# A quarter of some softmax subtractions on ACT and POOL, attention keys spread by DMA, and transposes moved ahead on TensorE

## The chip, the cores and the metric

The kernel runs on one core of a Trainium2 chip. The metric is the device time of one execution in microseconds. The engines are named as in the profile: PE (TensorE), DVE (VectorE), ACT (ScalarE), POOL (GpSimd) and SP (SyncE, which here only issues DMA transfers). All arithmetic is in float32.

## The reference

A sequence of 128 batches of 64 tokens with 128 channels goes through four layers. What matters here are their five attentions, each with 16 heads of 8 channels over 64 keys: L0s (self) and L0c (against a context), L1c (context), L2s (self) and L2c (context). After L0c and after L2c comes an MLP; L3 is a mixture of three experts that the change doesn't touch. Cut to one attention:

```python
def _attend(q, k, v):
    attn = jnp.einsum('bhnd,bhsd->bhns', q, k) * SCALE
    attn = jax.nn.softmax(attn, axis=-1)
    o = jnp.einsum('bhns,bhsd->bhnd', attn, v)
    return o.transpose(0, 2, 1, 3).reshape(B, N, D)
...
xm = _ln(x) * (1.0 + sc_sa) + sh_sa
qkv = (xm @ qkv_w + qkv_b).reshape(B, N, 3, H, HD)
...
x = x + g_sa * (_attend(q, k, v) @ sa_proj_w + sa_proj_b)     # L0s
x = x + _attend(q, k, v) @ ca_proj_w + ca_proj_b              # L0c: k, v from the context
```

The gates (`g_sa` and the like) are rows of one value per batch and channel, computed once from a condition vector.

## The kernel before

**Tiling.** The 8192 tokens are 16 groups (`NST`) of 8 batches, that is 512 tokens. A group's activations x stay in SBUF as 128 tokens by 4 tiles by 128 channels. Each attention stage runs over the 16 groups, one after the other, and the five stages follow in the order above. The list of all groups of a run of stages is what `attend` gets as `ats`.

**Halves and steps.** The scores of a group are computed in two halves of 4 batches, u = 0 and u = 1. `step(k)` emits one half's worth of work, and it does so for three halves at once: the scores of half k (`scores`), the transposes and exponentials of half k-1 (`turned`, twice, for the first and the second pair of head groups), and the weighted sums of half k-2 (`weighted`). In between it advances two lists of generators: `prepare` (for later groups: load, statistics, norm, transposes `psT`, their eviction into `cm` or `xm`, the key product `pk`, the query product `pq`, the value product `pvv`) and `finish` (for earlier groups: sums of the exponentials, their reciprocals, the output projection `py` and the addition into x). Each `go(prep, i)` or `go(fin, i)` runs a generator to its next `yield`. The schedule is manual: every engine executes its instructions in the order in which they are written out, and waits at an instruction whose semaphores aren't there, with all that follows on that engine behind it.

**Scores.** 16 heads are 4 groups g of 4 heads j. The keys of a group lie 4 times in `kbd`, once for each head j, with the rows of the other heads zero: POOL makes them with four products by a mask of 0 and 1 (L444). The scores `sc` take 4 banks of PSUM, 2048 columns, one bank for each g; there is one such buffer. DVE takes the maximum of each row of 64 (`mx`, L485) and subtracts it into SBUF (`e`, L487). PE turns `e` by transposes (`pp`, L503; 2 banks, one buffer), ACT takes the exponential while it evicts them (`eT`, L507), and PE multiplies with the values `vbd` (`po`, L520), which carry a column of ones for the sums.

**PSUM.** Of the 8 banks, 4 are `sc`, 2 `pp`, and 2 are the pool `mm`, from which `po`, `pk`, `pq`, `psT`, `pvv` and `py` all take their buffers. A new tile there waits until the tile that had its bank before has been read out.

**Eviction of the transposes.** In self groups and in L1c ACT evicts `psT` in eight pieces with scale and bias of the batch (L359, 2.47 us for the eight); in L0c and L2c it is one copy (L379, 0.58 us).

**Finish.** SP moves the rows of sums to DRAM (`sums`) and back with another shape (`rc`), and moves half of `o` to other partitions (L545, four transfers). DVE takes the reciprocal, `recs` goes to DRAM, and `rb` comes back broadcast over the channels of each head (L554); self groups also load a tile of gates (`gt`, L278). POOL multiplies (`oT`, L557), PE projects (`py`, L563), and DVE adds into x (L565 in cross groups; L568 and POOL in self groups).

**The first microseconds.** Weights and x come in by one queue on SP; DVE makes the statistics and the norm of the first group, and the products with the mask.

Of the kernel before, what the change touches and what calls it, by code (L numbers as in the profile page):

```python
# [15 lines left out]
P = 128  # L16
NST = 16
TT = 4
# [17 lines left out]
for _name, _n in _VECS:  # L36
# [13 lines left out]
    "L3_xcond_router_W": (3, 3), "L3_xcond_e_w1": (9, 256), "L3_xcond_e_w2": (6, 128),  # L50
    "L3_xcond_gate_w1": (3, 128), "L3_xcond_gate_w2": (1, 128), "L3_xcond_out_w": (1, 128),
}
_RAW = [
    "x", "cond_1024", "ctx_1024", *_WTS,
    "L0_xcond_ca_proj_b", "L1_xcond_bp", "L2_xcond_b_cproj", "L3_xcond_router_b", "L3_xcond_e_b2",
# [4 lines left out]
def tile_kernel(ctx: ExitStack, tc: tile.TileContext, a: dict, out: bass.AP):  # L60
# [15 lines left out]
    nc.sync.dma_start(cond, a["cond_1024"])  # L76
    vec_rows = const([_NVEC, P], "vec_rows")
    nc.scalar.dma_start(vec_rows, a["vecs"])
    mask = const([P, 4], "mask")
    nc.scalar.dma_start(mask, a["mask"])  # L80

    w = {}

    def load_weights(prefix, pool=cp):
        for name, (k, n) in _WTS.items():
            if name.startswith(prefix):
                t = pool.tile([P, k, n], F32, tag=name, name=name)
                src = a[name]
                if len(src.shape) == 3:
                    src = src.rearrange("e c n -> (e c) n")  # L90
                nc.sync.dma_start(t, src.rearrange("(k p) n -> p k n", p=P))
                w[name] = t

    xs = [const([P, TT, P], f"x{s}") for s in range(NST)]
# [23 lines left out]

    ident = const([P, P], "ident")
    make_identity(nc, ident)  # L120
    nhalf = const([P, TT], "nhalf")
    G.memset(nhalf, -0.5)

# [43 lines left out]
        Places.ak.tile([P, NB, 8, 32], F32, tag=f"vbd{i}", name=f"vbd{i}", bufs=1) for i in range(2)  # L167
    ]

    def clear(t):  # L170
        G.memset(t, 0.0)
        G.memset(t[0:L, :, :, 16:17], 1.0)
        G.memset(t[L:P, :, :, 17:18], 1.0)


# [2 lines left out]
    condT = const([P, P], "condT")  # L178
    scT = const([P, P], "scT")
    mods = {}  # L180

    def col(name, i=0):
        r = _ROW[name] + i
# [20 lines left out]

    def folded_column(wp, bp, bv, i):
        pb = mm("pb")
        T.matmul(pb[:, 0:1], w[wp][:, 0], col(bv, i), start=True, stop=True)
        t = const([P, 1], "pb_" + wp)
        V.tensor_add(t, pb[:, 0:1], col(bp))
        proj_bias[wp] = t  # L210
# [3 lines left out]
    def gate_table(wmod, wp, i=2, bias=None):  # L214

        table = dp.tile([P, 2, P], F32, tag="gate_" + wp, name="gate_" + wp)
        rows = const([P, 2, P], "gate_rows")
        gb = const([P, P], "gate_bias")
        V.tensor_scalar_mul(gb, mods[wmod][:, i, :], proj_bias[wp] if bias is None else bias)

        def second():
            pg = mm("pg")
            for q, src in enumerate((mods[wmod][:, i, :], gb)):
                T.transpose(pg[:, ts(q, P)], src, ident)
            V.tensor_copy(rows, pg[:, 0 : 2 * P].rearrange("p (i c) -> p i c", i=2))
            nc.sync.dma_start(table, rows)
            gates[wp] = table

        return second

    def folded_row(wp, bp, bv):
        bvs = const([P, P], "bvs")
        V.tensor_copy(bvs, col(bv, 1).broadcast_to([P, P]))

        def second():
            pb = mm("pb")
            T.matmul(pb[:, :P], bvs, w[wp][:, 0], start=True, stop=True)
            V.tensor_add(row_bias[bp], row_bias[bp], pb[:, :P])
            proj_bias[wp] = row_bias[bp]

        return second

    def condition():
        pc = mm("pc")
        T.transpose(pc[:, :P], cond, ident)
        V.tensor_copy(condT, pc[:, :P])
        S.activation(scT, pc[:, :P], AF.Silu)
        pv = mm("pv")
        T.transpose(pv[:, :_NVEC], vec_rows, ident[:_NVEC, :_NVEC])
        V.tensor_copy(vec, pv[:, :_NVEC])  # L250
        V.tensor_scalar_add(vec1, vec, 1.0)

    first_mods = modulations("L0_xcond_adaln_w", "L0_xcond_adaln_b", 6, (1, 4))
# [19 lines left out]
    def gate_tile(pool, s, wp):  # L273

        gt = pool.tile([P, TT, 2, P], F32, tag="gt", name="gt")
        for h in range(2):
            r = gates[wp].rearrange("(s t h) i c -> s h t (i c)", t=TT, h=2)[s, h]
            nc.sync.dma_start(  # L278
                gt[ts(h, L)].rearrange("p t i c -> p t (i c)"),
                r.unsqueeze(0).broadcast_to([L, TT, 2 * P]),  # L280
            )
        return gt

# [97 lines left out]

    turn = [0]

    ctxT = dp.tile([NST, P, NT], F32, tag="ctxT", name="ctxT")

    def prepare(pools, at):
# [16 lines left out]
        if cross:  # L403
            cn = c
            if layer != "L0c":
                cn = pool.tile([P, TT, P], F32, tag="cn", name="cn", bufs=1)
                for t in range(TT):
# [4 lines left out]
                    else:  # L412
                        S.activation(cn[:, t, :], c[:, t, :], AF.Identity, bias=nb, scale=rs)
        yield
        if layer == "L1c":
            kv_in = modulated_by_batch(pool, transposed(psum, cn), "L1_xcond_Wss_kv", 0, 1, s, "cm")
        elif cross:
            kv_in = copied(pool, transposed(psum, cn), "cm")
            if layer == "L0c":
                nc.sync.dma_start(ctxT[s], kv_in)  # L420
        else:
            q_in = kv_in = modulated_by_batch(
                pool, transposed(psum, xn), at["wmod"], 1, 0, s, by_dve=at.get("first", False)
            )
        yield
        if not cross:
# [12 lines left out]
        i = turn[0] % 2  # L439
        turn[0] += 1  # L440
        vbd = vbds[i]
        kbd = pool.tile([P, 4, NB, L], F32, tag="kbd", name="kbd")
        for j in range(4):
            (V if at.get("first") else G).tensor_scalar(  # L444
                kbd[:, j], by_batch(kT), mask[:, j : j + 1], 1.0, ALU.mult, ALU.mult
            )
        yield
        pq = psum.tile([P, 512], F32, tag="mm", name="pq")
        T.matmul(pq, at["wq"], q_in, start=True, stop=True)  # L449
# [11 lines left out]
                    start=True, stop=True,  # L461
                )
        pv4 = pvv.rearrange("p b (i d) -> p b i d", d=HD)
        S.copy(vbd[0:L, :, :, 0:HD], pv4[0:L])
        S.copy(vbd[L:P, :, :, HD : 2 * HD], pv4[L:P])
        at["vbd"] = vbd

    def scores(pools, at, u):
# [5 lines left out]
        for t2 in range(2):  # L474
# [9 lines left out]
        mx = pool.tile([P, 32], F32, tag="mx", name="mx")  # L484
        V.tensor_reduce(mx, sc.rearrange("p g (m k) -> p (g m) k", k=L), AX.X, ALU.max)  # L485
        e = pool.tile([P, 32, L], F32, tag="e", name="e")
        V.tensor_tensor(  # L487
            e, sc.rearrange("p g (m k) -> p (g m) k", k=L),
            mx.unsqueeze(2).broadcast_to([P, 32, L]), ALU.subtract,
        )  # L490
        return e

    def turned(pools, e, eT, gg):

# [35 lines left out]
    def finish(pools, at):  # L530
# [3 lines left out]
        cross = at["layer"][2] == "c"  # L534

        sums = dp.tile([16, NT], F32, tag="sums", name="sums", bufs=2)
        for j in range(2):
            nc.sync.dma_start(
                sums.rearrange("(g i j) t -> j g i t", i=2, j=2)[j], o[16 + j : P : 32, :, :]
            )  # L540
        rc = pool.tile([P, L], F32, tag="rc", name="rc")
        nc.sync.dma_start(rc, sums.rearrange("h (c t) -> (h c) t", t=L))

        for g in range(4):
            nc.sync.dma_start(o[32 * g + 16 : 32 * g + 32, 0, :], o[32 * g : 32 * g + 16, 1, :])  # L545
        yield
        V.reciprocal(rc, rc)
        recs = dp.tile([16, NT], F32, tag="recs", name="recs", bufs=2)
        nc.sync.dma_start(recs.rearrange("h (c t) -> (h c) t", t=L), rc)

        if not cross:
            gt = gate_tile(pool, s, at["wp"])
        rb = pool.tile([P, NT], F32, tag="rb", name="rb", bufs=1)
        nc.sync.dma_start(rb, recs.unsqueeze(1).broadcast_to([16, HD, NT]))  # L554
        yield
        oT = pool.tile([P, NT], F32, tag="oT", name="oT", bufs=1)
        G.tensor_tensor(oT, o[:, 0, :], rb, ALU.mult)  # L557
# [13 lines left out]
    def attend(pools, ats):  # L571
# [16 lines left out]
        def step(k, between=(), late=()):  # L588
            i, u = divmod(k, 2)
            now, last, past = (  # L590
                halves[k - d] if 0 <= k - d < 2 * n else None for d in range(3)
            )
            if now:
                now["e"] = scores(pools, now["at"], now["u"])
            for f in between:
                f()
            if last:
# [1 line left out]
                turned(pools, last["e"], last["eT"], 0)  # L599
            if past:  # L600
                weighted(pools, past["at"], past["u"], past["eT"])
            if u == 0:
                go(fin, i - 2)
                go(prep, i + 4)
                go(prep, i + 1)
                go(fin, i - 3)
            else:
                go(prep, i + 1)
            if last:
                turned(pools, last["e"], last["eT"], 1)  # L610
            if u == 0:
                go(prep, i + 2)
                go(prep, i + 3)
            else:
                go(prep, i + 1)
                go(prep, i + 2)
                for f in late:
                    f()
                go(fin, i - 1)
                go(fin, i - 2)  # L620
                go(prep, i + 4)
# [3 lines left out]
    def attention_of(s, layer):  # L625
        if layer[2] == "s":
            wmod, wqkv, bqkv, wp = {
                "L0s": ("L0_xcond_adaln_w", "L0_xcond_qkv_w", "L0_xcond_qkv_b", "L0_xcond_sa_proj_w"),
                "L2s": ("L2_xcond_W_mod", "L2_xcond_W_qkv", "L2_xcond_b_qkv", "L2_xcond_W_proj"),
            }[layer]  # L630
            m = w[wqkv][:, 0]
            return dict(
                s=s, layer=layer, wmod=wmod, wp=wp, wq=m[:, 0:P], bq=col(bqkv, 0),
                wk=m[:, P : 2 * P], bk=col(bqkv, 1), wv=m[:, 2 * P : 3 * P],
            )
        wq, bq, wkv, bkv, wp = {
            "L0c": (
# [8 lines left out]
        }[layer]  # L646
        m = w[wkv][:, 0]
        return dict(
            s=s, layer=layer, wp=wp, wq=w[wq][:, 0], bq=col(bq), wk=m[:, 0:P], bk=col(bkv, 0),
            wv=m[:, P : 2 * P],  # L650
        )

# [537 lines left out]
    def stages():  # L1190
# [41 lines left out]
        clear(vbds[0])  # L1232
        ahead_1(0, 1, 2, 3)
        condition()
        ahead_1(0, 0)
        first_mods[0]()
        ahead_1(0, 0, 1, 2, 0, 0, 1)
# [11 lines left out]
            f()  # L1249
        first_mods[2]()  # L1250
        n = last + 2 + len(heads_0)
        for f in steps_1[6:-n]:
            f()
        for s in range(2):
            heads_0[3 + s] = lambda s=s, f=heads_0[3 + s]: (f(), load_context(s))
        rest = into_mlp(steps_1, heads_0, turns_0)
# [68 lines left out]
```

## Time and profile before

The profiled execution took 1626.31 us in all; its span, from the first to the last instruction, is 1624.5 us. The three timed runs have a median of 1624.67 us (1624.43 to 1626.63).

| what | us |
| --- | --- |
| median of the runs | 1624.67 |
| profiled execution, its span | 1626.31, 1624.5 |
| busy in the span: PE, DVE, POOL, ACT | 1573.8, 1240.4, 1072.5, 1035.5 |
| L0s, from its first maximum to that of L0c (16.94 to 210.47) | 193.5 |
| from the first maximum of L0c to that of L1c (210.47 to 544.51), the first MLP with it | 334.0 |
| L1c (544.51 to 739.11) | 194.6 |
| L2s (739.11 to 931.28) | 192.2 |
| L2c, second MLP and L3 (931.28 to the end) | 693.2 |

The times of the stages are the starts of the 160 maxima (L485) in the timeline: one for each half, so that every second one starts a group. A line of the timeline has the start and the duration in us, the engine, the line of the kernel, what is written from what, the shapes, and how many instructions were merged; in brackets stands how long the engine had been idle and what ended that. The granted clock of TensorE is 0.997 of full speed on average. A matmul of 32-bit data shows as two records.

### The profile page before, as it was taken

To read this page: it belongs to the slowest core of one execution; us is meant where nothing else is said; L and a number is where in the kernel's file an instruction comes from. 1 tells how busy PE (TensorE), PEld (TensorE's weight loads), DVE (VectorE), ACT (ScalarE), POOL (GpSimd) and SP (SyncE) were. 2 spreads that over 40 slices of the span, in tenths; PEclk is the share of its full clock that TensorE was granted. 3 is DMA by queue.
4 is the path that set the end of the run, shared out by engine and by line. 5 is a ranking of instruction groups with operands and counts; after the bars stand their busy time and mean duration, and the time that the engine had idled before them with its cause. 6 is when DMAs were issued, how large, how long until landed. Compare 5 with 4: busy or idle time off the path is not lost.

```text
span 1624.5 us, 64028 instructions
## 1 busy us (share of the span) xinstructions
PE 1573.8 (97%) x27842; PEld 1086.8 (67%) x27842; DVE 1240.4 (76%) x1566; ACT 1035.5 (64%) x1710; POOL 1072.5 (66%) x1786
## 2 busy tenths in 40 slices
PE   6999999998999899999999999998999999999998
PEld 4676777776544577776777777776777566666665
DVE  7898998898555688899899889896443566666666
ACT  5788777776433678878888888886334544444443
POOL 6687787766888789887787876775875333333322
PEclk9999999999999999999999999999999999999999
DMA  8334453332111022211334432222533111111100
GB/s 209 85 82 99 107 127 92 83 83 72 55 36 55 16 63 61 72 44 50 90 82 102 104 88 73 62 56 59 130 81 76 31 39 37 40 33 36 34 12 19
DMA packets 146775, 112.65 MB, mean 69 GB/s; under 512 B 36357, under 2 KB 125247, under 8 KB 146495
## 3 DMA queue, kind: packets, MB, share of 16 engines
q1 hardware_dynamic: 146288, 108.53, 26.1%
q8 instruction: 219, 3.59, 0.9%
q14 instruction: 61, 0.50, 0.1%
q10 hardware_dynamic: 207, 0.03, 0.0%
HBM read 83.99 MB, written 14.02 MB: 60 GB/s over the span
## 4 chain that ended last, share of the span: by engine, by line
PE 83%; DVE 12%; ACT 3%; issue 1%; DMA 0%; SPq 0%; DVEq 0%
PE sc L478 10%; PE pp L503 9%; PE po L520 7%; PE ph L693 7%; PE ph L1080 6%; PE ph L1081 6%; DVE e L487 6%; DVE mx L485 6%; PE po L1111 5%; PE psT L342 5%; PE pk L436 5%; PE py L563 4%; PE py L709 4%; PE py L699 3%; PE pvv L459 3%; PE pq L449 3%
## 5 line engine op out<-in xcount | busy, mean ns | idle before, releaser
L507 ACT ACTIVATE eT<-pp 128x1024 f32<-128x1024 f32 x320 | 329.7, 1030 | 160.8 <-PE pp L503 160.7
L485 DVE TENSOR_REDUCE mx<-sc 128x32 f32<-128x2048 f32 x160 | 366.6, 2291 | 83.6 <-PE sc L478 83.6
L487 DVE TENSOR_TENSOR e<-sc,mx 128x2048 f32<-128x2048 f32 x160 | 366.6, 2291 | 5.4
L503 PEld LDWEIGHTS pp<-ident,e 64*128 64x128 f32 x5120 | 183.9, 138 | 140.1 <-ACT eT L507 44.7
L503 PE MATMUL pp<-ident,e 64*128 64x64 f32 x5120 | 227.7, 229 | 7.2 <-DVE e L487 4.7
L444 POOL TENSOR_SCALAR kbd<-kT,mask 128x512 f32<-128x512 f32 x316 | 212.4, 690 | 31.3 <-ACT kT L438 28.3
L372 POOL TENSOR_SCALAR xn<-x,nmu,rs 128x128 f32<-128x128 f32 x508 | 223.6, 453 | 13.3
L557 POOL TENSOR_TENSOR oT<-o,rb 128x512 f32<-128x512 f32 x80 | 102.1, 1276 | 163.5 <-DMA rb<-recs 62.9
L478 PE MATMUL sc<-kbd,qT 32*64 32x256 f32 x5120 | 179.2, 387 | 16.6 <-DVE e L487 15.6
L694 ACT ACTIVATE h<-ph,vec 128x512 f32<-128x512 f32 x128 | 87.3, 687 | 149.9 <-PE ph L693 149.7
L520 PE MATMUL po<-eT,vbd 128*32 128x64 f32 x10240 | 178.1, 221 | 1.4 <-issue 1.3
L1087 ACT ACTIVATE h<-h 128x512 f32<-128x512 f32 x112 | 70.6, 630 | 149.8 <-DVE h L1083 130.9
L520 PEld LDWEIGHTS po<-eT,vbd 128*32 128x32 f32 x10240 | 151.3, 110 | 14.4 <-issue 2.0
L330 POOL TENSOR_TENSOR rs<-rs,nhalf 128x4 f32<-128x4 f32 x128 | 130.2, 1017 | 10.7
L478 PEld LDWEIGHTS sc<-kbd,qT 32*64 32x64 f32 x5120 | 97.7, 131 | 53.0 <-issue 19.6
L1083 DVE TENSOR_TENSOR h<-ph,ab 128x512 f32<-128x512 f32 x112 | 76.9, 687 | 62.6 <-PE ph L1081 62.5
L1116 DVE SCALAR_TENSOR_TENSOR acc<-po,pr,acc 128x128 f32<-128x128 f32 x192 | 67.2, 350 | 44.1 <-PE po L1111 39.6
L1080 PE MATMUL ph<-nx,w 128*128 128x512 f32 x192 | 100.7, 607 | 0.0
L528 ACT COPY o<-po 128x512 f32<-128x512 f32 x160 | 95.7, 598 | 5.1 <-PE po L520 2.0
L1081 PE MATMUL ph<-u,w_ev 128*128 128x512 f32 x192 | 98.9, 597 | 0.0
L1111 PEld LDWEIGHTS po<-w_2o,h 128*128 128x128 f32 x768 | 92.1, 192 | 8.7 <-issue 8.4
L1104 POOL TENSOR_SCALAR g<-g 128x512 f32<-128x512 f32 x16 | 9.9, 622 | 132.1 <-ACT g L1103 132.1
(259 smaller groups left out, 2868.5 us busy)
## 6 DMA issues: line engine op xcount, KB each, us to landing
rb<-recs SPq DMA_DIRECT2D x80, 256.0 KB
c<-in_ctx_dram SPq DMA_DIRECT2D x64, 256.0 KB
o<-o SPq DMA_DIRECT2D x320, 32.0 KB
gt<-gate_L_xcond_sa_proj_w SPq DMA_DIRECT2D x32, 256.0 KB
gt<-gate_L_xcond_W_proj SPq DMA_DIRECT2D x32, 256.0 KB
gt<-gate_L_xcond_W_mlp SPq DMA_DIRECT2D x32, 256.0 KB
x<-in_x_dram SPq DMA_DIRECT2D x16, 256.0 KB
ctxT<-cm SPq DMA_DIRECT2D x16, 256.0 KB
```

Of the source, the lines that this page charges most:

```text
L330: G.tensor_tensor(rs, rs, nhalf, ALU.pow)
L372: engine.tensor_scalar(xn[:, t, :], src[:, t, :], nmu[:, t : t + 1], rs[:, t : t + 1], ALU.add, ALU.mult)
L444: (V if at.get("first") else G).tensor_scalar(kbd[:, j], by_batch(kT), mask[:, j : j + 1], 1.0, ALU.mult, ALU.mult)
L478: T.matmul(sc[ts(h, L), g, ts(t2, 256)], qT[ts(g, 32), ts(b, L)], kbd[ts(g, 32), :, b, :], start=True, stop=True,)
L485: V.tensor_reduce(mx, sc.rearrange("p g (m k) -> p (g m) k", k=L), AX.X, ALU.max)
L487: V.tensor_tensor(e, sc.rearrange("p g (m k) -> p (g m) k", k=L), mx.unsqueeze(2).broadcast_to([P, 32, L]), ALU.subtract,)
L503: T.transpose(pp[:, h, ts(4 * g2 + 2 * i + t2, L)], e6[ts(h, L), 2 * gg + g2, t2, i], ident[ts(h, L), ts(h, L)],)
L507: S.activation(eT[:, gg], pp, AF.Exp, scale=HD ** -0.5)
L520: T.matmul(po[ts(g, 32), i, ts(2 * t2 + h, L)], at["vbd"][:, 4 * u + 2 * t2 + h, 2 * g + i, :], e7[:, g // 2, h, g % 2, i, t2, :], start=T ...
L1080: T.matmul(ps, wn, d["nx"], start=True, stop=False)
L1081: T.matmul(ps, we, d["u"], start=False, stop=True)
L1111: T.matmul(po[:, ex, :], d[q][:, ts(t, P)], k3["w_2o"][:, q, :], start=r == 0, stop=r == 1)
```

## The change

The heads within each group of four are interleaved by channel: row 4d + j instead of 8j + d of the 32 rows of a group. With that the following is done.

- `spread`: from the third group on, the keys come into two standing buffers `kbd` (zero where they are not written) by four DMA transfers on SP, of 32 partitions by 2 KB each, in place of the four products on POOL. To that end the columns of the query and key weights are reordered once, those of L0s by DVE at the start (`reorder(V, ...)`), the others by POOL beside L0s; bias vectors come in three orders, the projection weights are loaded with reordered rows, and the mask is made by DVE from the identity.
- `scores`: where `shared_with_pool` says so (second halves, and both halves in L0c and L2c), DVE subtracts the maxima only in 3 of the 4 banks. `rest` copies the fourth by ACT and subtracts by POOL. In a step `rest` stands after the weighted sums and ahead of the key or query product.
- `prepare`: the transposes `psT` of the group after next are emitted in a first half ahead of the second `turned`, their eviction behind it (`in_two`, `open`); before, both stood behind it.
- `finish`: the gate tile and `rb` are loaded one generator step after `recs`; the tables of gates are stored so that a tile's row is contiguous; one transfer instead of two collects the sums, one instead of four moves half of `o`, and two instead of one bring `rb`.

The core of the diff:

```diff
@@ load_weights
-                nc.sync.dma_start(t, src.rearrange("(k p) n -> p k n", p=P))
+                if name in _TURNED:
+                    of = src.rearrange("(g i r) n -> i g r n", i=2, r=2 * HD)
+                    for i in range(2):
+                        nc.sync.dma_start(t[i:P:2, 0, :], of[i])
+                else:
+                    nc.sync.dma_start(t, src.rearrange("(k p) n -> p k n", p=P))
...
+    kbds = [
+        Places.ak.tile([P, 4, NB, L], F32, tag=f"kbd{i}", name=f"kbd{i}", bufs=1) for i in range(2)
+    ]
...
+    def reorder(engine, name, n):
+        for i in range(n):
+            t = const([P, P], "gate_bias")
+            cols = w[name][:, 0, ts(i, P)]
+            engine.tensor_copy(t.rearrange("p (g d j) -> p g d j", d=HD, j=4), by_element(cols))
+            engine.tensor_copy(cols, t)
...
@@ gate_tile
-            r = gates[wp].rearrange("(s t h) i c -> s h t (i c)", t=TT, h=2)[s, h]
+            r = gates[wp].rearrange("(s h t) i c -> s h (t i c)", t=TT, h=2)[s, h]
             nc.sync.dma_start(
-                gt[ts(h, L)].rearrange("p t i c -> p t (i c)"),
-                r.unsqueeze(0).broadcast_to([L, TT, 2 * P]),
+                gt[ts(h, L)].rearrange("p t i c -> p (t i c)"),
+                r.unsqueeze(0).broadcast_to([L, TT * 2 * P]),
             )
...
+    def spread(kbd, kT):
+        for j in range(4):
+            nc.sync.dma_start(kbd[j:P:4, j].rearrange("p b l -> p (b l)"), kT[j:P:4, :])
...
@@ prepare
         yield
+        ps = transposed(psum, cn if cross else xn)
+        if at.get("in_two"):
+            at["open"] = True
+            yield
+            at["open"] = False
         if layer == "L1c":
-            kv_in = modulated_by_batch(pool, transposed(psum, cn), "L1_xcond_Wss_kv", 0, 1, s, "cm")
+            kv_in = modulated_by_batch(pool, ps, "L1_xcond_Wss_kv", 0, 1, s, "cm")
...
-        kbd = pool.tile([P, 4, NB, L], F32, tag="kbd", name="kbd")
-        for j in range(4):
-            (V if at.get("first") else G).tensor_scalar(
-                kbd[:, j], by_batch(kT), mask[:, j : j + 1], 1.0, ALU.mult, ALU.mult
-            )
+        kbd = kbds[i]
+        if turn[0] <= 2:
+            for j in range(4):
+                (V if at.get("first") else G).tensor_scalar(
+                    kbd[:, j], by_batch(kT), mask[:, j : j + 1], 1.0, ALU.mult, ALU.mult
+                )
+        else:
+            spread(kbd, kT)
...
@@ scores
+        n = 24 if shared_with_pool(at, u) else 32
         V.tensor_tensor(
-            e, sc.rearrange("p g (m k) -> p (g m) k", k=L),
-            mx.unsqueeze(2).broadcast_to([P, 32, L]), ALU.subtract,
+            e[:, 0:n], sc[:, 0 : n // 8].rearrange("p g (m k) -> p (g m) k", k=L),
+            mx[:, 0:n].unsqueeze(2).broadcast_to([P, n, L]), ALU.subtract,
         )
-        return e
+
+        def rest():
+            if n < 32:
+                S.copy(e[:, n:32], sc[:, 3].rearrange("p (m k) -> p m k", k=L))
+                G.tensor_tensor(
+                    e[:, n:32], e[:, n:32],
+                    mx[:, n:32].unsqueeze(2).broadcast_to([P, 32 - n, L]), ALU.subtract,
+                )
+
+        return e, rest
+
+    def shared_with_pool(at, u):
+        return u == 1 or at["layer"] in ("L0c", "L2c")
...
@@ finish
-        for j in range(2):
-            nc.sync.dma_start(
-                sums.rearrange("(g i j) t -> j g i t", i=2, j=2)[j], o[16 + j : P : 32, :, :]
-            )
+        nc.sync.dma_start(sums.rearrange("(m i) t -> m i t", i=2), o[1:P:16, :, :])
...
-        for g in range(4):
-            nc.sync.dma_start(o[32 * g + 16 : 32 * g + 32, 0, :], o[32 * g : 32 * g + 16, 1, :])
+        nc.sync.dma_start(o[1:P:2, 0, :], o[0:P:2, 1, :])
...
+        yield
         if not cross:
             gt = gate_tile(pool, s, at["wp"])
         rb = pool.tile([P, NT], F32, tag="rb", name="rb", bufs=1)
-        nc.sync.dma_start(rb, recs.unsqueeze(1).broadcast_to([16, HD, NT]))
+        for i in range(2):
+            r = recs.rearrange("(m i) t -> i m t", i=2)[i]
+            nc.sync.dma_start(rb[i:P:2, :], r.unsqueeze(1).broadcast_to([8, HD, NT]))
...
@@ step
             if past:
                 weighted(pools, past["at"], past["u"], past["eT"])
+            if rest:
+                rest()
             if u == 0:
+                go(prep, i + 1)
                 go(fin, i - 2)
                 go(prep, i + 4)
-                go(prep, i + 1)
+                go(fin, i - 2)
                 go(fin, i - 3)
+                if i + 2 < n:
+                    ats[i + 2]["in_two"] = True
+                go(prep, i + 2)
             else:
                 go(prep, i + 1)
             if last:
                 turned(pools, last["e"], last["eT"], 1)
             if u == 0:
-                go(prep, i + 2)
+                if i + 2 < n and ats[i + 2].get("open"):
+                    go(prep, i + 2)
                 go(prep, i + 3)
...
@@ stages
         condition()
+        reorder(V, "L0_xcond_qkv_w", 2)
...
-        for f in steps_1[6:-n]:
+        for i, f in enumerate(steps_1[6:-n]):
             f()
+            if i % 2 and i // 2 < len(names):
+                reorder(G, *names[i // 2])
```

## The prediction

> **What bounds the kernel now.** I read the page's busy table and the chain that ended last first, then the timeline of one group in each attention stage, then the built order of the changed kernel with its semaphore waits (a build, no time in it). The page:
>
> ```profile
> span 1624.5 us, 64028 instructions
> PE 1573.8 (97%) x27842; PEld 1086.8 (67%) x27842; DVE 1240.4 (76%) x1566; ACT 1035.5 (64%) x1710; POOL 1072.5 (66%) x1786
> L485 DVE TENSOR_REDUCE mx<-sc 128x32 f32<-128x2048 f32 x160 | 366.6, 2291 | 83.6 <-PE sc L478 83.6
> L487 DVE TENSOR_TENSOR e<-sc,mx 128x2048 f32<-128x2048 f32 x160 | 366.6, 2291 | 5.4
> ```
>
> PE is nearly full. DVE never overlaps its maximum with the next scores, because there is one score buffer: scores, maximum, subtraction and the next scores are a ring. A second half in L0s (the `sc` lines open and close it):
>
> ```profile
> 143.38 1.12 PE L478 MATMUL sc<-kbd,qT 32*64 32x256 f32 x32
> 143.83 2.47 ACT L359 ACTIVATE xm<-psT,mod_L_xcond_adaln_w 128x64 f32<-128x64 f32 x8
> 144.61 2.29 DVE L485 TENSOR_REDUCE mx<-sc 128x32 f32<-128x2048 f32 x1 [0.54 <-PE sc L478]
> 146.35 1.12 PE L449 MATMUL pq<-xm,L_xcond_qkv_w 128*128 128x512 f32 x2 [0.18 <-ACT xm L359]
> 146.94 2.29 DVE L487 TENSOR_TENSOR e<-sc,mx 128x2048 f32<-128x2048 f32 x1
> 147.04 0.64 ACT L528 COPY o<-po 128x512 f32<-128x512 f32 x1
> 147.51 0.76 ACT L451 ACTIVATE qT<-pq,vec 128x512 f32<-128x512 f32 x1
> 148.16 1.03 ACT L507 ACTIVATE eT<-pp 128x1024 f32<-128x1024 f32 x1
> 149.37 1.12 PE L478 MATMUL sc<-kbd,qT 32*64 32x256 f32 x32 [0.18 <-DVE e L487]
> ```
>
> It takes 5.99 us: 1.23 from scores to maximum, 2.33 to the subtraction, 2.29 for that, 0.14 back to PE. ACT has hardly a gap either, and `pq` waits for ACT (`xm`). A first half in L0c, and the start of its second:
>
> ```profile
> 281.34 1.12 PE L478 MATMUL sc<-kbd,qT 32*64 32x256 f32 x32
> 282.57 2.29 DVE L485 TENSOR_REDUCE mx<-sc 128x32 f32<-128x2048 f32 x1 [0.80 <-PE sc L478]
> 284.89 2.29 DVE L487 TENSOR_TENSOR e<-sc,mx 128x2048 f32<-128x2048 f32 x1
> 285.02 1.08 PE L563 MATMUL py<-L_xcond_ca_proj_w,oT 128*128 128x128 f32 x8
> 285.22 0.69 ACT L438 ACTIVATE kT<-pk,vec 128x512 f32<-128x512 f32 x1 [0.40 <-PE pk L436]
> 286.03 0.71 PE L503 MATMUL pp<-ident,e 64*128 64x64 f32 x16
> 286.67 0.66 PE L342 MATMUL psT<-ident,c 128*128 128x128 f32 x4
> 287.10 0.54 DVE L547 RECIPROCAL rc<-rc 128x64 f32<-128x64 f32 x1
> 287.26 1.12 PE L478 MATMUL sc<-kbd,qT 32*64 32x256 f32 x32
> 287.56 0.63 DVE L565 TENSOR_TENSOR x<-x,py 128x512 f32<-128x512 f32 x1
> ```
>
> Here PE has no gap at all: each matmul group starts as the last ends (first half 5.92 us, second 6.09). By the starts of the maxima a group takes 11.92 us in L0s and L2s, 12.01 in L0c and L2c, 12.25 in L1c (5.92 + 6.33); 16 groups each. So shorter DVE work can buy little: PE's own starts in an L0s second half add to 5.50 (1.05+0.64+1.03+1.06+0.64+1.08), a floor of 11.42 per self group, 12.0 per cross group.
>
> **The change, part by part.** Halves with a shared bank are every second half, and both in L0c and L2c.
>
> *Subtraction.* The DVE part has 1536 of 2048 columns: the 256-column form of the same operation (L988) takes 0.425 us, so 0.425 + 1280 x (2.291-0.425)/1792 = 1.76, 0.53 less. The fourth bank is an ACT copy (rows of 128x512 copies: 0.58 to 0.60) and a POOL subtraction in SBUF (L348, a broadcast operand, 1.04; L557 1.28). But in the built order the ACT copy waits for the DVE subtraction of the same tile `e`, in all 112 cases. It stands between the `o` copy and `qT` (second half) or `kT` (first half), so ACT stands still with `qT`, `kT` and the second exp behind it.
> The Trainium skill ("PSUM — Partial Sum Buffer", Specifications) says that ACT and DVE read PSUM side by side at full rate in different banks. By that the copy would be free beside the subtraction and the change about 40 us better than my sum; the built order doesn't let it start.
>
> *Transposes ahead of the second `pp`.* They take 0.64 us of PE before `pp` instead of after it, so the second exp, and on ACT's queue the eviction of `psT` behind it, come 0.64 later. The buffer also changes hands: in the built order of L0c and L2c `psT` gets the bank that `py` has just left, freed by the DVE add into x (L565), where it was `pk`'s, freed by `kT`.
>
> Self stages (L0s, L2s). First half: as before, 5.94 (whole subtraction). Second half, two paths. PE: `pq` waits for `xm`, which ends 0.64 later; from `pq` to the next scores is 149.37-146.35 = 3.02, so 2.97+0.64+3.02 = 6.63. ACT: 1.23+2.33+1.76 = 5.32, +0.06 to the copy, +0.58, less 0.10 overlap, `qT` 0.72, 0.08 to PE, for the scores wait for `qT`: 6.66. Take 6.66: +0.68 per group, x28 = 19.0; the last two groups of each stage prepare cross groups whose `psT` adds 0.6 in that half: +1.1 x 4 = 4.4.
>
> L1c. First half unchanged. Second half: `qT` ends at 6.58, the query transposes wait for its buffer (they did before, without harm), 0.10, and 0.58 to the scores: 7.25 against 6.33, +0.92 x14 = 12.9; the last two groups have none, +0.7 x2 = 1.4.
>
> L0c, L2c. First half: 1.23+2.32, then `rc` starts 1.68 after the subtraction, the add 0.46 later, 0.63: 6.32; 0.10, `psT` 0.59, `pp` 0.64: scores at 7.65, +1.73. Second half as in L1c: 7.25, +1.16. Together 2.89 x 28 groups = 80.9 (the last two of each stage prepare nothing: +0.3 x4 = 1.2).
>
> *Keys by transfers.* Four POOL products of 0.69 go (2.7 us per group, off the path) for four 64 KB transfers on SP behind `kT`. An issue costs SP 0.56 to 0.83 (the four `o` moves took 2.49 to 3.45), so recs and rb, behind them, go out 0 to 1.1 later. SP loses four issues elsewhere (three `o`, one sums) and gains one (rb in two). Cover: in L0s `kT` ends about 4.8 after the first scores, issues end by 8.1, and recs to rb, a write and its receipt, was 2.24 (131.64 to 133.88), so keys are there by 11, needed at 12.6. rb: landed 4.6 to 5.6 after its issue, `oT` ready some 2.8 after the first scores, needed by `py` at 3.7 on PE; the group grows by 0.7, and 1.6 us are left. I take 0; if the cover goes, up to 1.3 per self group. POOL's subtraction is done 1.3 after the copy and first read 4 us later: 0; the products that POOL loses gain nothing, as the list of waits has nobody waiting for POOL's `kbd`. Gate tables in two, fewer and longer rows: 0, their landing is waited for by nobody in the chain.
>
> *Start.* The reordering of the qkv columns (four 128x128 copies, as the `xn` row 0.28 each) stands on DVE ahead of the first statistics, and waits for a weight that is 192 KB behind the one that PE got at 5.80; at 334 GB/s (windows, 4 to 8 us) some 6.4. Statistics at 7.5 instead of 4.69: +2.8, bounds +1.1 (only the copies) and +4 (landing at 7.6). The later POOL reorderings take the place of the freed products: 0.
>
> **Sum.** 2.8+19.0+4.4+12.9+1.4+80.9+1.2 = 122.6. The profiled execution took 1626.31 (span 1624.5): 1748.9; the median of the runs is 1.64 lower: 1747.
>
> **Rivals.** (B) The copy costs nothing beyond its length, ACT finds its bank early: self second halves still 6.63 by PE, L1c +0.64, cross only +1.73: 28x0.64+4x0.6+16x0.64+28x1.73+2.8 = 82, so 1706. For it: the data would allow it; against it: the wait in all 112 places. (C) Faster: the ring is 0.53 shorter and nothing on ACT or in the buffers binds. Then PE's floor decides: self -0.48x32, L1c -0.25x16, the last halves before the MLPs some -5, start +2.8: -22, so 1603. It needs the copy started before the DVE subtraction ends, and `psT` not waiting for the add; the built order is against both. (D) SP becomes the bound: dearer key issues and 256 KB more per group beside gates and rb make `oT` late by 1.3 in 28 self groups: +36, 1783. For it: rb already comes only 0.9 us before it is needed. (E) No net change (gains in self stages pay for the cross stages) would need cross groups under 12.5; the add alone sets 7.65 for a half.
>
> **How the numbers follow.** Chances: forecast 0.77, D 0.09, B 0.08, C 0.04, E 0.02. About 0.2% (3 us) can be told from no change. Range 1710 to 1782: down to nearly B, up to nearly D, which also takes in a fifth of the sum either way. Faster 0.04, same 0.02, slower 0.94.
>
> **What would show it.** Starts of the maxima 12.6 us apart in L0s and L2s, 13.2 in L1c, 14.9 in L0c and L2c; the ACT copy starting within 0.1 us of the end of the subtraction, idle before it put down to DVE e; `psT` in L0c and L2c waiting for the add into x, PE's busy share falling to some 90%; subtraction at 1.76; first maximum at 19.7 instead of 16.94; MLPs and L3 unchanged. Wrong if the copy starts before the subtraction ends, if transposes in L0c start within 5 us of the scores, or if POOL `oT` waits for rb with `py` behind it.

## The result and the profile after

The changed kernel takes 1763.06 us (median of 4 runs, 1761.18 to 1766.74) against 1625.65 us of the kernel before beside it: 1.0848 times as long, 95% interval 1.0827 to 1.0869. Forecast were 1747 us, with a range of 1710 to 1782. The page of the changed kernel (busy time, the chain that ended last, and the groups of instructions: busy us and mean ns, then idle us before them and what ended it):

```profile
span 1762.2 us, 64146 instructions
PE 1597.7 (91%) x27844; PEld 1094.8 (62%) x27844; DVE 1184.1 (67%) x1575; ACT 1085.0 (62%) x1822; POOL 987.0 (56%) x1602
...
PE 61%; DVE 25%; ACT 6%; DMA 3%; issue 2%; SPq 1%; POOL 1%; DVEq 0%; ACTq 0%; POOLq 0%
...
L555 DVE TENSOR_REDUCE mx<-sc 128x32 f32<-128x2048 f32 x160 | 366.7, 2292 | 245.8 <-PE sc L548 239.5
L558 DVE TENSOR_TENSOR e<-sc,mx 128x1536 f32<-128x1536 f32 (+1 forms) x160 | 306.9, 1918 | 5.4
L565 ACT COPY e<-sc 128x512 f32<-128x512 f32 x112 | 65.7, 586 | 146.1 <-DVE e L558 146.1
```

DVE has 56 us less work than before, and yet its maximum waits 239.5 us for the scores where it waited 83.6: the ring has become longer, not shorter. PE is busy 91% instead of 97%. And the new copy on ACT, 0.586 us each, has stood still 146.1 us before it ran, all of it put down to the DVE subtraction. The list of waits (us in total, times, longest) of the same kernel adds where PE and POOL stood:

```profile
ACT e L565 <- DVE e L558: 146.1, 112, 2.7
POOL oT L639 <- DMA rb<-recs: 79.4, 49, 3.6
PE psT L398 <- DVE x L647: 39.3, 24, 2.0
PEld py L645 <- POOL oT L639: 34.2, 46, 2.4
```

A first half in L0c, from its scores to those of the second, in the timeline of PE, DVE and ACT:

```profile
275.16 1.12 PE L548 MATMUL sc<-kbd,qT 32*64 32x256 f32 x32
...
278.78 1.76 DVE L558 TENSOR_TENSOR e<-sc,mx 128x1536 f32<-128x1536 f32 x1
...
280.46 0.54 DVE L626 RECIPROCAL rc<-rc 128x64 f32<-128x64 f32 x1
280.63 0.59 ACT L565 COPY e<-sc 128x512 f32<-128x512 f32 x1 [1.98 <-DVE e L558]
280.92 0.63 DVE L647 TENSOR_TENSOR x<-x,py 128x512 f32<-128x512 f32 x1
281.11 0.69 ACT L505 ACTIVATE kT<-pk,vecp 128x512 f32<-128x512 f32 x1
...
281.60 0.65 PE L398 MATMUL psT<-ident,c 128*128 128x128 f32 x4 [1.68 <-DVE x L647]
282.19 0.71 PE L586 MATMUL pp<-ident,e 64*128 64x64 f32 x16
...
282.83 1.12 PE L548 MATMUL sc<-kbd,qT 32*64 32x256 f32 x32
```

It takes 7.67 us where it took 5.92. The copy starts 0.09 us after the subtraction ends, after 1.98 us of idle ACT, with `kT` behind it; `psT` waits 1.68 us for the add into x, and `pp` and the scores follow it on PE. A second half in L0s, from the subtraction to the next scores:

```profile
147.57 1.76 DVE L558 TENSOR_TENSOR e<-sc,mx 128x1536 f32<-128x1536 f32 x1
...
149.42 0.59 ACT L565 COPY e<-sc 128x512 f32<-128x512 f32 x1 [0.57 <-DVE e L558]
149.90 0.69 ACT L521 ACTIVATE qT<-pq,vecp 128x512 f32<-128x512 f32 x1
...
150.65 1.12 PE L548 MATMUL sc<-kbd,qT 32*64 32x256 f32 x32 [0.29 <-ACT qT L521]
```

Subtraction, copy, `qT`, scores: each begins when the one before it ends. By the starts of the maxima, with the sum's terms beside them:

| stage | median group before, after | longer by | the sum had |
| --- | --- | --- | --- |
| to the first maximum | 16.94, 20.20 (its start) | 3.3 | 2.8 |
| L0s | 11.92, 12.65 | 17.4 | 11.7 |
| L0c with the first MLP | 12.01, 14.88 | 46.8 | 41.1 |
| L1c | 12.25, 13.11 | 16.1 | 14.3 |
| L2s | 11.92, 12.60 | 11.5 | 11.7 |
| L2c to its last maximum | 12.00, 14.89 | 44.5 | 41.1 |
| rest | | -1.9 | 0 |
| sum | | 137.7 | 122.6 |

The period of an undisturbed group is what the prediction said, to 0.1 us, in all five stages. What is missing lies in single groups (they also lift the median of L0s, where the undisturbed ones take 12.60).

### The profile page after: what moved, and what is told of

Its sections match the earlier page's. It is cut to its first block, busy times and chain, and to the rows that moved or that the text cites. A ratio compares the mean times of both kernels' runs of the same rounds, so it can differ in the third digit from the quotient of the medians.

```text
span 1762.2 us, 64146 instructions
## 1 busy us (share of the span) xinstructions
PE 1597.7 (91%) x27844; PEld 1094.8 (62%) x27844; DVE 1184.1 (67%) x1575; ACT 1085.0 (62%) x1822; POOL 987.0 (56%) x1602
## 4 chain that ended last, share of the span: by engine, by line
PE 61%; DVE 25%; ACT 6%; DMA 3%; issue 2%; SPq 1%; POOL 1%; DVEq 0%; ACTq 0%; POOLq 0%
DVE mx L555 13%; PE sc L548 9%; DVE e L558 9%; PE ph L783 6%; PE ph L1170 6%; PE ph L1171 5%; PE psT L398 5%; PE po L1201 5%; PE pp L586 4%; PE py L799 3%; PE py L789 3%; PE po L603 3%; PE py L645 3%; PE pk L503 3%; ACT e L565 2%
## 5 line engine op out<-in xcount | busy, mean ns | idle before, releaser
L555 DVE TENSOR_REDUCE mx<-sc 128x32 f32<-128x2048 f32 x160 | 366.7, 2292 | 245.8 <-PE sc L548 239.5
L558 DVE TENSOR_TENSOR e<-sc,mx 128x1536 f32<-128x1536 f32 (+1 forms) x160 | 306.9, 1918 | 5.4
L566 POOL TENSOR_TENSOR e<-e,mx 128x512 f32<-128x512 f32 x112 | 116.8, 1043 | 305.7 <-ACT e L565 305.4
L586 PEld LDWEIGHTS pp<-ident,e 64*128 64x128 f32 x5120 | 187.8, 141 | 156.3 <-ACT eT L590 100.3
L586 PE MATMUL pp<-ident,e 64*128 64x64 f32 x5120 | 232.2, 232 | 14.1 <-ACT eT L590 9.5
L548 PE MATMUL sc<-kbd,qT 32*64 32x256 f32 x5120 | 186.7, 400 | 19.5 <-ACT qT L521 10.5
L565 ACT COPY e<-sc 128x512 f32<-128x512 f32 x112 | 65.7, 586 | 146.1 <-DVE e L558 146.1
L398 PE MATMUL psT<-ident,xn 128*128 128x128 f32 x512 | 81.3, 282 | 35.8 <-ACT qT L521 29.7
```

Source lines behind the costliest of these rows:

```text
L398: T.transpose(ps[:, ts(t, P)], src[:, t, :], ident)
L548: T.matmul(sc[ts(h, L), g, ts(t2, 256)], qT[ts(g, 32), ts(b, L)], kbd[ts(g, 32), :, b, :], start=True, stop=True,)
L558: V.tensor_tensor(e[:, 0:n], sc[:, 0 : n // 8].rearrange("p g (m k) -> p (g m) k", k=L), mx[:, 0:n].unsqueeze(2).broadcast_to([P, n, L]), ...
L586: T.transpose(pp[:, h, ts(4 * g2 + 2 * i + t2, L)], e6[ts(h, L), 2 * gg + g2, t2, i], ident[ts(h, L), ts(h, L)],)
```

## The experiments

All are edits of the changed kernel, apart from the last two. Each has its expectation as it was on record before the run.

**1. A buffer of its own for the copy.** The prediction said that the copy waits because it writes the same tile `e` as the subtraction.

```diff
-                S.copy(e[:, n:32], sc[:, 3]...)
-                G.tensor_tensor(e[:, n:32], e[:, n:32], mx...)
+                e3 = pool.tile([P, 32 - n, L], F32, tag="y", name="e3")
+                S.copy(e3, sc[:, 3]...)
+                G.tensor_tensor(e[:, n:32], e3, mx...)
```

> The kernel after with one edit: ACT's copy of the fourth bank goes into a buffer of its own, and POOL subtracts from that into `e`. Theory A (the prediction's words: the copy waits because it writes the same tile `e` as the DVE subtraction): the copy starts when the `o` copy is done, some 1 to 2 us earlier, second halves lose ACT's path, and the time falls by some 40 us to about 1722. Rival (the wait belongs to the two readers of the score tile `sc`, for the built order still has the copy behind the DVE subtraction, in all 111 places that name it): no change, 1763 within 4 us, the copy's idle time still put down to DVE e.

Measured: 1762.02 us, ratio 1.0837 (1.0813 to 1.0861). The wait in the list of this kernel:

```profile
ACT e L566 <- DVE e L558: 142.3, 111, 2.3
```

It is the wait of before, in another buffer. So `e` was not what tied the two; the rival holds.

**2. Only second halves shared.**

```diff
-        return u == 1 or at["layer"] in ("L0c", "L2c")
+        return u == 1
```

> The kernel after with only second halves shared: first halves of L0c and L2c subtract all four banks on DVE again. In this built order `psT` of those halves takes pk's bank again and waits for ACT kT instead of the DVE add into x. Theory (the largest term of the sum, +1.73 us in each of 28 first halves, comes from the copy ahead of kT and from the bank that py leaves): these halves go back to 5.9 to 6.2 us, the time falls by 40 to 48 us, to about 1718. Rival (the transposes ahead of the second pp stretch them by themselves): at least 1745.

Measured: 1710.78 us, ratio 1.0514 (1.0495 to 1.0534). First halves of L0c and L2c are back at 5.90 us (7.60), second ones stay at 7.21 (7.28). In such a first half `psT` has no wait left:

```profile
285.49 0.66 PE L398 MATMUL psT<-ident,c 128*128 128x128 f32 x4
```

The time falls by 52 us, 4 more than the upper end expected; 28 x 1.70 is 48. The transposes stand ahead of `pp` here as well, so they don't stretch this half by themselves.

**3. No sharing at all.** `n = 32` in every half; the rest of the change stays.

> The kernel after without any sharing (DVE subtracts all four banks everywhere); keys by transfers, gates in two, and the transposes ahead of the second pp stay. Theory (most of the loss is ACT's wait for the subtraction and the bank that changes hands with it): left are the start and the first groups 7, self second halves 6.63 by PE (28 x 0.66 = 18, last groups 4), late rb some 5, and 0 to 0.6 in each cross half pair (0 to 27): 1660 to 1687, about 1668. Rival (the transposes are the main loss): 1720 or more. Starts of the maxima: 12.6 us apart in L0s, 12.0 to 12.5 in L0c.

Measured: 1667.17 us, ratio 1.0249 (1.0229 to 1.0269). So 96 of the 137 us come with the sharing. The median group takes 12.58 us in L0s and 12.17 in L0c, the undisturbed ones 12.19 and 12.08. Second halves of L2s take 6.30 us, not the 6.63 that the prediction had for PE's path: `xm` comes only 0.54 later than before, not 0.64, and from `pq` to the scores it is 2.78 rather than 3.02; most of this difference is the 0.18 us that the scores waited for the subtraction before.

**4. The score buffer as two tiles.** If readers of one tile are put in order, then a tile for the one bank that ACT reads must free the copy, whichever buffer it writes.

```diff
-        sc = psc.tile([P, 4, 512], F32, tag="sc", name="sc")
+        sc = psc.tile([P, 3, 512], F32, tag="sc", name="sc")
+        s3 = psc.tile([P, 512], F32, tag="s3", name="s3")
...
-        V.tensor_reduce(mx, sc, ...)
+        V.tensor_reduce(mx[:, 24:32], s3, ...)
+        V.tensor_reduce(mx[:, 0:24], sc, ...)
```

> The kernel after with the score buffer as two tiles, three banks and one: the maximum of the one bank is a DVE instruction of its own and comes first, and ACT's copy reads that tile. In the built order the copy then waits for that maximum alone, and psT in L0c and L2c for kT. Theory: the copy is over before the subtraction ends, and what is left is the start 7, two more DVE instructions in each of 48 halves that aren't shared (0.43 each, 21), the transposes' 0.64 in second halves (self 28 x 0.66 + 4 = 23, L1c 10), 0.6 to 1.2 per cross group (17 to 34), late rb 5: 83 to 100 over before, 1708 to 1725. Rival (the copy's own 0.6 us on ACT and the work given to POOL are the cost, not the wait): 1750 or more.

Measured: 1666.00 us, ratio 1.0244 (1.0221 to 1.0267): 97 us less, below the expected 1708. The group of copies in its page:

```profile
L572 ACT COPY e<-s 128x512 f32<-128x512 f32 x112 | 69.4, 620 | 0.8 <-DVE mx L557 0.8
```

The same 112 copies, the same POOL subtractions, 208 DVE instructions more: 0.8 us of idle instead of 146.1. A first half in L0c now:

```profile
274.54 0.59 ACT L572 COPY e<-s 128x512 f32<-128x512 f32 x1
274.84 1.08 PE L652 MATMUL py<-L_xcond_ca_proj_w,oT 128*128 128x128 f32 x8
274.84 1.76 DVE L561 TENSOR_TENSOR e<-sc,mx 128x1536 f32<-128x1536 f32 x1
275.04 0.69 ACT L505 ACTIVATE kT<-pk,vecp 128x512 f32<-128x512 f32 x1
...
275.79 0.65 PE L398 MATMUL psT<-ident,c 128*128 128x128 f32 x4
```

The copy starts before the subtraction does, and `psT` follows `py` with no wait. With the copy early, the built order also gives `psT` the bank that `pk` had again, freed by `kT`; it is no longer the add into x that it needs. The expectation was too high because it kept 0.6 to 1.2 us per cross group and 0.43 per unshared half; the group of L0c takes 12.15 us, and an unshared first half 6.05.

**5. The transposes back behind the second `pp`,** sharing kept.

```diff
-                if i + 2 < n:
-                    ats[i + 2]["in_two"] = True
-                go(prep, i + 2)
...
-                if i + 2 < n and ats[i + 2].get("open"):
-                    go(prep, i + 2)
+                go(prep, i + 2)
```

> The kernel after with the transposes of the group after next back behind the second pp; the sharing stays, with its waits. Theory (with the copy waiting, the transposes' place matters only where psT stands in front of pp): self and L1c stay at 12.6 and 13.1 us per group, since there the path over ACT's copy and qT ends last; in L0c and L2c the first half loses psT's 0.6 us, 28 x 0.6 = 17: about 1746, 1740 to 1752. Rival (both parts cost for themselves and add): what the sharing alone costs, 1763 less the 40 that are left without it, so 1723 or less.

Measured: 1746.35 us, ratio 1.0735 (1.0719 to 1.0751). First halves of L0c take 6.96 us, 0.64 less; second halves stay, 7.28 there and 6.63 in L0s, so in those ACT's path over copy and `qT` ends last, whatever PE does.

**6. Neither sharing nor transposes ahead.** What is left is keys, gates and sums by other transfers, and the permuted columns.

> The kernel after without sharing and with the transposes behind the second pp: what is left of the change is keys by transfers, gates in two, sums and rb in other transfers, the permuted columns and their reordering at the start. Theory: the start 2.5 to 3.3, a late rb in a few groups 3 to 8, nothing else: 1630 to 1640. Rival (the four key transfers per group on SP cost the 40 us of the run without sharing): 1655 to 1668.

Measured: 1652.64 us, ratio 1.0156 (1.0139 to 1.0173). The theory fails: 27 us are left, and only 3.4 of them are there at the first maximum. First halves are irregular, 5.9 to 8.0 us and one of 9.6, mostly where `oT` comes late. In the list of waits:

```profile
POOL oT L639 <- DMA rb<-recs: 217.8, 45, 9.7
PEld py L645 <- POOL oT L639: 56.0, 59, 2.9
```

SP's queue ahead of such a half, and `oT` in it:

```profile
74.17 3.53 SPq L444 DMA_DIRECT2D kbd<-kT  x4
77.80 0.53 SPq L628 DMA_DIRECT2D recs<-rc  x1
78.37 1.13 SPq L334 DMA_DIRECT2D gt<-gate_L_xcond_sa_proj_w  x2
79.61 1.27 SPq L636 DMA_DIRECT2D rb<-recs  x2
...
85.87 1.27 POOL L639 TENSOR_TENSOR oT<-o,rb 128x512 f32<-128x512 f32 x1 [5.60 <-DMA rb<-recs]
```

The reciprocal was done at 75.86, but `recs` goes out at 77.80, behind four key transfers.

**7. Two score tiles and the transposes behind.**

> The kernel after with the score buffer as two tiles (as in the run with that edit alone) and the transposes behind the second pp. Theory (the copy no longer waits, and the transposes' place costs about what it costs without sharing): second halves lose 0.2 to 0.5 each, 74 of them, 15 to 30: 1636 to 1651. If the sharing then pays at all, it is below the run with neither. Rival (the two parts need each other: the freed time goes to the transposes): 1660 to 1670.

Measured: 1648.86 us, ratio 1.0136 (1.0104 to 1.0168). Its four runs lie 11 us apart (1642.6 to 1653.2), and its interval overlaps that of run 6: sharing without the wait has no cost there that could be measured, and no gain either. Shared second halves of L0s take 5.68 us (5.93), but unshared first halves, where DVE now has four instructions, 6.05 where nothing disturbs them (5.93), and up to 7.7 where they are irregular, as in run 6.

**8. POOL's key products again, in the changed kernel.**

```diff
-        if turn[0] <= 2:
+        if True:
```

> The kernel after with the keys as POOL's four masked products in every group again, not four transfers. Theory (the key transfers stand in SP's queue before recs and rb and make oT late in a few groups): oT's idle time on rb falls from 79 us to below the 63 of before, py's wait for oT nearly goes, 5 to 12 us less, 1751 to 1758. Rival (POOL's products, 2.7 us per group, now delay POOL's subtraction or oT): 1763 or more.

Measured: 1756.53 us, ratio 1.0814 (1.0784 to 1.0845). The late `rb` is gone:

```profile
POOL oT L639 <- DMA rb<-recs: 7.0, 10, 1.5
```

The theory holds, and its size: 6.5 us, though the intervals of the two kernels overlap. Of its four runs three took 1755.4 to 1757.6 us, and the profiled one 1766.3; that one shows why, and it is the subject of run 9. Its first halves in L0c take 7.60 to 7.67 and 8.06 to 8.53 in turn, up to the tenth group. One of the long ones on PE, and the granted clock around it (PEclk is the third number from the end):

```profile
311.13 0.71 PE L586 MATMUL pp<-ident,e 64*128 64x64 f32 x16
311.78 1.99 PE L548 MATMUL sc<-kbd,qT 32*64 32x256 f32 x32
313.70 1.11 PE L586 MATMUL pp<-ident,e 64*128 64x64 f32 x16
```

```profile
312.00:313.00 1.00, 1.00 (x24) 0.71 (x24) 0.00 (x0) 1.00 (x2) 1.00 (x2) 0.50 0.67 200
313.00:314.00 1.00, 1.00 (x22) 0.30 (x8) 0.16 (x1) 0.39 (x1) 1.00 (x3) 0.50 0.44 152
314.00:315.00 1.00, 1.00 (x28) 0.88 (x28) 1.00 (x1) 0.08 (x1) 0.90 (x3) 0.50 0.82 295
315.00:316.00 1.00, 1.00 (x64) 0.91 (x56) 1.00 (x1) 0.94 (x1) 0.95 (x3) 0.86 0.16 61
```

The scores take 1.99 us instead of 1.12: the clock was at half for some 3.4 us. This profile has 18 such stretches, the changed kernel's 11, that of before 3.

**9. PE's idle time filled.** In every group of L0c and L2c of kernel 8 the second `pp` is written two more times ahead of `psT`.

```diff
+                if last and last["at"]["layer"] in ("L0c", "L2c"):
+                    pp = turned(pools, last["e"], last["eT"], 1, again=2)
```

> The kernel with POOL's key products (the run of that edit), and in every group of L0c and L2c the sixteen transposes of the second pp issued two more times, ahead of psT: 1.28 us more of PE work per group, in the 1.68 us in which PE waits there for the DVE add into x; the same values are written, and psT still waits for the same add. Theory (the granted clock falls to 0.50 for 3.5 us in every second group of these stages because PE stands idle there, and each such stretch makes the half 0.9 us longer): more work and less time, the stretches at 0.50 in L0c and L2c go, halves of 8.4 to 8.5 us become 7.6, 12 times 0.9: 1744 to 1750. Rival (the clock falls for another reason): as many low stretches, 1754 to 1764.

Measured: 1755.71 us, ratio 1.0782 (1.0764 to 1.0799). `psT` now has 0.54 us of idle before it:

```profile
304.61 1.21 PE L586 MATMUL pp<-ident,e 64*128 64x64 f32 x32
306.36 0.66 PE L398 MATMUL psT<-ident,c 128*128 128x128 f32 x4 [0.54 <-DVE x L649]
```

Profile against profile the theory holds: 6 stretches at half clock, in L0c and L2c only one each, in the first group, which is the one that gets no extra transposes (the `pp` written in its first half belongs to the stage before); the first halves of all the other full groups there take 7.60 to 7.67; the span is 1752.8 instead of 1764.5, although PE has 1024 transposes more. The mean clock of its four runs is 0.995 to 0.996, against 0.982 to 0.991. But the median is the same as of kernel 8, in the range that was given for the rival, so the expected 1744 to 1750 is missed: the profiled run of kernel 8 was the unlucky one. The three others have a mean clock of 0.990 to 0.991, by which they had some ten stretches and not 18 (an estimate: 0.0095 of 1754 us, at 1.7 us lost in each). Where these lay isn't shown, and why they cost so little stays open.

**10. Run 6 with POOL's key products.**

> The kernel with neither sharing nor the transposes ahead, and the keys as POOL's products again; the gates in two, sums, rb in two, the permuted columns and the start stay. Theory (the key transfers, ahead of recs and rb in SP's queue, make rb late by 0.3 to 2 us in about 20 first halves): those go, the first maximum stays at 19 to 20.4, and 1652.6 becomes 1627 to 1634. Rival (the other transfers or the new order of the steps make rb late): 1645 or more, py still waiting for oT some 50 us in all.

Measured: 1632.62 us, ratio 1.0029 (1.0018 to 1.0040). The key transfers are 20 of the 27 us. The same group as above, and then the waits:

```profile
76.09 0.33 SPq L628 DMA_DIRECT2D recs<-rc  x1
77.80 1.27 SPq L636 DMA_DIRECT2D rb<-recs  x2
82.57 1.28 POOL L639 TENSOR_TENSOR oT<-o,rb 128x512 f32<-128x512 f32 x1 [1.05 <-DMA rb<-recs]
```

```profile
POOL oT L639 <- DMA rb<-recs: 119.3, 44, 9.1
PEld py L645 <- POOL oT L639: 22.2, 31, 1.5
```

`recs` goes out 1.71 us earlier than in run 6, `rb` 1.81 and `oT` 3.30. So only about half of the delay is the place in SP's queue; the other 1.5 us passed between the issue of `rb` and its arrival, with the key transfers issued shortly before, and no run takes that part by itself. The idle time of `py` on `oT` is 22.2 us (56.0).

**11. The kernel before, with the score buffer as two tiles and all halves shared,** and nothing else.

> The kernel before with one change alone: the score buffer as two tiles (three banks and one, the maximum of the one bank first), and the fourth bank less its maxima by POOL from ACT's copy in every half, the copy behind the o copy. Keys, transfers and transposes as before. Theory (what the sharing is worth when the copy doesn't wait): second halves in L0s and L2s go from 5.98 to 5.68, as in the run with two tiles and the transposes behind, the rest stays at PE's 5.9 and 6.1: 32 x 0.3 = 10 less, 1612 to 1619. Rival (ACT, 1.2 us more per group, takes back what the ring gives): 1624 or more.

Measured: 1630.23 us, ratio 1.0011 (0.9999 to 1.0023), the rival's number, but not by ACT. L2s gains 0.25 us per group (11.67), and L1c loses 1.1 (13.37). The window of one group of L1c, with the busy us of PE, PEld, DVE, ACT and POOL:

```profile
642.03:655.40 13.37, 12.31 (x309) 8.77 (x308) 10.06 (x9) 10.44 (x21) 12.99 (x21) 1.00 0.22 59
```

POOL works 12.99 of 13.37 us, and `py` waits for its `oT`. L1c is where POOL also has norms and modulations to do.

**12. The same, but DVE keeps the fourth bank in first halves of L1c.**

```diff
+        own = at["layer"] == "L1c" and u == 0
...
+        if own:
+            V.tensor_tensor(e[:, 24:32], s3, by_8, ALU.subtract)
```

> The kernel before with the score buffer as two tiles and the fourth bank by ACT's copy and POOL, as in the run with that change alone, except in first halves of L1c, where DVE subtracts that bank too. Theory (POOL was full in L1c: 12.99 us of work in a group of 13.37): a group of L1c loses POOL's 1.04 and goes from 13.37 to 12.3, 14 x 1.07 = 15 less than 1630.2: 1612 to 1619, faster than before by 0.5 to 0.9%. Rival (in L1c the two more DVE instructions of the first half take the place of POOL): 1624 or more.

Measured: 1620.09 us, ratio 0.9949 (0.9936 to 0.9962): faster than both kernels, by 0.5% against before, 1 us above the expected. L1c is at 12.28 us per group. Copy and subtraction in L0s:

```profile
116.92 1.76 DVE L491 TENSOR_TENSOR e<-sc,mx 128x1536 f32<-128x1536 f32 x1
116.93 0.59 ACT L501 COPY e<-s 128x512 f32<-128x512 f32 x1
```

They run at the same time, each as long as it is alone. That agrees with the Trainium skill ("PSUM — Partial Sum Buffer", Specifications), which has ACT and DVE read different banks side by side at full rate. The banks were never what kept the copy back.

## Why the prediction was right, and where it wasn't

**The copy's wait.** Right in place and size: 112 times, 146 us of idle, the copy 0.1 us after the subtraction, second halves of L0s at 6.63 (6.66 said), of L1c at 7.22 (7.25). Run 5 shows that it is ACT's path that sets the second halves, run 4 that without the wait 97 of the 137 us go. The reason given for it was wrong: not "the same tile `e`" (run 1), but two readers of the one tile `sc`, which the build puts in order (run 4). That the sum's two paths for a second half came out nearly alike, 6.66 by ACT and 6.63 by PE, was chance: PE's alone takes 6.30 (run 3), and the 6.63 measured is ACT's.

**The bank of `psT`.** Right: 7.60 and 7.28 us in L0c and L2c (7.65 and 7.25 said), `psT` after the add. The prediction booked it as a consequence of the transposes' new place; runs 3 and 4 show that it comes with the copy's wait: with the transposes in the same place, and no copy or an early one, `psT` doesn't wait. Run 5 shows what their place adds while the copy waits, 17 us as expected. Without sharing, run 3 less run 6, it is 14.5 us.

**Rival B (the copy costs only its length), 1706.** Run 4 is its condition made true, and gives 1666. The rival's sum kept 28 x 1.73 for the bank, 48 us, and these go together with the copy's wait.

**Keys by transfers: "I take 0".** This is the step that failed; rival D's mechanism, though not its size. The prediction gave `oT` 1.6 us of slack. Runs 6 and 10 put the transfers at 20 us where groups are short (12.0), and run 8 at some 6.5 us in the changed kernel, where longer groups cover most of it. The waits before:

```profile
POOL oT L557 <- DMA rb<-recs: 62.9, 21, 8.7
PEld py L563 <- POOL oT L557: 13.9, 22, 1.6
```

After, `oT` waits for `rb` in 49 groups, and `py` for `oT` 34.2 us: the last of the signs by which the prediction said it would be wrong came true. One reading under it was wrong too: the 2.24 us from `recs` to `rb`, taken for a write and its receipt, hold two issues of the gate tile (1.76 us from 132.01 on), so they don't tell what a receipt takes.

**The rest of the 15 us that the sum lacks.** The start took 3.3 for 2.8 in the profile (over the profiles of its variants the first maximum lies anywhere from 19.1 to 20.5). The last two groups of L0c took 13.66 and, in the first half of the last, 6.79, where the sum had 0.3 more than 12.10 and 5.90 each. Half-clock stretches aren't in the sum at all: three halves of L2c took 8.44 to 8.50 for 7.60 with such a stretch, and the second half of the second group of L0s, 8.86 where it was 6.88 before, has one too (8.00 in run 2, without one). These are single groups read from one profile; no run took them apart.

## What to carry to other kernels

Before work on one PSUM tile is given to two engines, look in the built order at what the second reader waits for: where readers of a tile are put in order, as here, they run one after the other, whatever banks they read, and a tile of its own for each reader's banks removes the wait. A wait on ACT is paid by all that stands behind it, and it can change which buffer a later tile gets. A transfer that takes work from another engine isn't free if its issues stand in a queue ahead of a transfer that is needed soon, and an engine's slack must be counted in each stage by itself, as POOL's in L1c.

## What the hardware showed that was not expected

PE's clock falls to half for about 3.4 us after waits far shorter than that: 1.68 us of idle before `psT` is enough, but not every time. In the profile of run 8 it is every second group of L0c up to the tenth, with stretches that start at 250.4, 281.2, 311.9, 342.6 and 373.3 us. A half in which one falls on the scores is 0.9 us longer. The starts are 30.7 us apart, nine times 3.41, as if the clock were set anew only at the ends of fixed windows of 3.41 us. By such windows PE was busy for 1.73 or 1.74 us, about half, in the window ahead of each of these stretches, and for 2.4 us or more in every window of run 9's full groups behind the first in L0c and L2c, where there is no stretch. Half busy is not enough by itself: 414.28 to 417.69 in run 8 has 1.73 us and no stretch behind it. The Trainium skill ("TensorE: Matmul & The Clock Gate", What's actually happening) tells of a free-running window of 3.4 us after which the clock is halved if PE was idle through it. The half clock, the length of the stretches and the spacing of their starts agree; the idle time doesn't, since PE was busy for half of the window.
